# Other blocks for GpSimd's part of the softmax sums, and the steps that wait for GpSimd placed by an estimate of its queue

## The chip, the cores and the metric

The kernel runs on one core of a Trainium2 chip. The metric is the device time of one execution in microseconds, and the time of a version is the median of several runs. A core has engines that work side by side, each through its own queue of instructions in order: TensorE (matrix products; "PE" in the profile, with its weight loads as "PEld"), VectorE ("DVE"), ScalarE ("ACT"), GpSimd ("POOL") and SyncE ("SP", which here only starts transfers). TensorE writes to PSUM[...]. Transfers (DMA) started by SP and by GpSimd share 16 DMA engines.

## What is computed

`x` holds 8 frames of 2048 nodes with 256 channels. A transformer layer with 8 heads of 32 channels works within each frame, an adjacency matrix masks the scores, and the whole is wrapped in one more residual and norm:

```python
qkv = x @ w_qkv                                   # q, k, v of 8 heads, 32 channels each
scores = q k^T / sqrt(32), -1e9 where adj == 0
t = softmax(scores) @ v
y = layernorm(x + t) * g1 + be1                   # first norm
h = relu(y @ w1 + b1)
z = layernorm(y + h @ w2 + b2) * g2 + be2         # second norm
out = layernorm(x + z)                            # third norm, without gain
```

Per frame and head that is a matrix of 2048 x 2048 scores, so attention is nearly all of the work.

## The kernel before, in words

**Tiling.** For a frame `f`, a chunk `qc` of 512 query nodes and a half `g` of the heads (4 heads), the scores are made transposed, a block `mb` of 128 key nodes at a time. One such block is an *item*: 8 frames x 4 chunks x 2 halves x 16 blocks = 1024 items. 16 items of one `(f, qc, g)` are a *group*, 32 are a chunk, 128 are a frame. The main loop takes one item per step `t`. In a step it issues, in this order: fill work (`advance`), the exponential of item `t+1` on ScalarE (`exponentials`, L237), the score products of item `t+2` on TensorE and the mask's addition on VectorE (`scores`, L230 and L233), the products of item `t` with the values on TensorE (`values`, L249), and the summing of item `t` (`add_up`, L268 and L271).

**The tiles p.** VectorE writes an item's scores into a tile `p` of 1 MB (pool `pp`, 12 buffers), ScalarE turns them into exponentials in place, and TensorE multiplies them with the values. Each `p` is also a part of the softmax's denominator. A matrix product with ones (L315) sums over the key nodes of one `p` in 8 instructions, and to spare TensorE 12 of a group's 16 blocks, they are first added together elsewhere:
- GpSimd adds the blocks of `POOLED` into the first of them, by a tensor addition (L271), 6 per group;
- DMAs that add at their target fold the blocks of the two chains `MOVED` into the first block of each (L268), issued by GpSimd, 6 per group. One link of a chain waits until the link before it has landed, since both write the same tile, and that wait stands in GpSimd's queue;
- the block `ALONE` goes to TensorE as it is.

TensorE then takes four terms per group (`denominator`): `ALONE`, the heads of the two chains, and the head of `POOLED`. A tile `p` comes free when its last reader is done: GpSimd's addition, the DMA's landing, or TensorE's product.

**The chunk's rest.** When the denominators of both halves are there, `outcome` divides (L353), adds `x` by a DMA that GpSimd issues (L339), and `tail` follows: the first norm (statistics on VectorE L278, the power on GpSimd L283 to L287, the scaling on ScalarE L290), transposes and the two feed-forward products on TensorE, the gain and the bias rows on GpSimd (L459, L461), the residual's addition on VectorE (L483), the second norm, its gain and bias rows on GpSimd (L363, L365), the addition of `x` by a DMA from GpSimd (L367), the third norm, and the store from SP (L370). At most two tails are under way at once. The last chunk has a version of its own in halves (`finish`).

**What sets the order.** All of this is written as Python generators that a planner resumes when the program is built; nothing of it is decided on the chip. A generator yields a number of steps to stay away, or `BANK` when it wants TensorE and the one free PSUM bank for fill work. `advance` keeps a credit of TensorE time per step, so that about one piece of fill work (a term of a denominator, a projection, a transpose, a part of the feed-forward) goes into each step, and takes the piece that is due first. Where a generator stays away too short a time, its next instruction stands in its engine's queue before its operand is there, and that engine waits, with all that is behind it.

In the kernel before, these distances are fixed numbers: 2 steps from the power on GpSimd to the scaling on ScalarE, 7 steps from the DMA at L367 to the third norm, a start of the first norm 16 steps after the chunk's last item, and `SUM = 4` steps after a group's last item until the term of `POOLED`.

```python
    POOLED = (0, 3, 6, 8, 11, 13, 15)
    MOVED = ((1, 4, 7, 10), (2, 5, 9, 12))
    ALONE = 14
...
        late = {len(blocks) - 1: ready}
...
            start(t + 2, denominator(f, qc, g, t + SUM), t + SUM + 4)
```

Of the kernel before, what the change touches and what calls it, by code (L numbers as in the profile page):

```python
# [28 lines left out]
SUM_MAX = 1e19  # L29
BANK, MORE, WAIT, TURNED, ROOM, INPUTS = -1, -2, -3, -4, -5, -10  # L30
STEP, UNIT, TURN, KEPT = 2200, 1024, 1400, 2200

MASKED = -57344.0
CODE = -5.0
# [27 lines left out]
def fast_path(ctx, tc, cst, x, adj, out, RS):  # L62
    nc = tc.nc
    F, N, C = x.shape
# [18 lines left out]
    ctx.enter_context(tc.manual_schedule())  # L83

    ident, identb, wqkv, w1s, w2s = cst["ident"], cst["identb"], cst["wqkv"], cst["w1s"], cst["w2s"]
    state = {"pair": 0, "side": None, "turn": 0, "turned": False, "holder": None, "tails": 0, "credit": 0}

    def columns(out, lhsT, rhs, start, stop):
        state["credit"] -= 4 * out.shape[-1]
# [164 lines left out]

    POOLED = (0, 3, 6, 8, 11, 13, 15)
    MOVED = ((1, 4, 7, 10), (2, 5, 9, 12))
    ALONE = 14

    ENDED = MB - 5
    SUM = 4

    def add_up(item):
        f, qc, g, mb = item
        for chain in MOVED:
            if mb in chain[1:] and not ((f, qc, g) == items[-1][:3] and mb >= ENDED):
                nc.gpsimd.dma_start(PT[f, qc, g, chain[0]], PT.pop(item), accum_op=ALU.add)  # L268
        if mb in POOLED[1:] and not ((f, qc, g) == items[-1][:3] and mb >= ENDED):
            first = PT[f, qc, g, POOLED[0]]  # L270
            nc.gpsimd.tensor_tensor(first, first, PT.pop(item), ALU.add)  # L271


    def norm(t, per=1):
        mv = small.tile([P, TPC, nc.vector.BN_AGGR_DIM], F32, name="mv")
        for j in range(TPC):
            st = small.tile([P, nc.vector.BN_STATS_DIM], F32, name="st")
            nc.vector.bn_stats(st, t[:, j, :])  # L278
            nc.vector.bn_aggr(mv[:, j, :], st)
            if j % per == per - 1:  # L280
                yield 1
        rs = small.tile([P, TPC], F32, name="rs")
        nc.gpsimd.tensor_scalar(rs, mv[:, :, 1], EPS, 1.0, op0=ALU.add, op1=ALU.mult)  # L283
        nc.gpsimd.tensor_tensor(rs, rs, cst["mhalf"], ALU.pow)  # L284
        nb = small.tile([P, TPC], F32, name="nb")
        nc.gpsimd.tensor_tensor(nb, mv[:, :, 0], rs, ALU.mult)
        nc.gpsimd.tensor_scalar(nb, nb, -1.0, 1.0, op0=ALU.mult, op1=ALU.mult)  # L287
        yield 2
        for j in range(TPC):
            nc.scalar.activation(t[:, j, :], t[:, j, :], AF.Identity, bias=nb[:, j:j + 1], scale=rs[:, j:j + 1])  # L290
            if j % per == per - 1:
                yield 1
# [1 line left out]
    def rows(v):  # L294
        return v[:, None, :].to_broadcast([P, TPC, C])

    def denominator(f, qc, g, ready):
        grp = (f, qc, g)
        blocks = [ALONE] + [chain[0] for chain in MOVED + (POOLED,)]
        late = {len(blocks) - 1: ready}  # L300
        if (f, qc, g) == items[-1][:3]:
            blocks = [POOLED[0], 11, 12, MOVED[1][0], 13, 14, MOVED[0][0], 15]
            late = {n: len(items) - k for n, k in ((2, 2), (3, 1), (4, 1), (5, 0), (6, 0), (7, 0))}
        yield BANK
        ps = bank()
        for n, block in enumerate(blocks):
            if n:
                yield MORE
            while state["now"] < late.get(n, 0):
                yield WAIT  # L310
            term = PT.pop((f, qc, g, block))
            state["credit"] -= 4 * CH
            for h in range(4):
                r = D * h
                nc.tensor.matmul(ps[r:r + D, :], cst["ones"], term[:, h, :], start=(n == 0), stop=(n == len(blocks) - 1))  # L315
# [12 lines left out]
        nc.vector.tensor_tensor(RS[:, 1], RS[:, 1], den, ALU.min)  # L328
        if g == 1:
            begin = items.index((f, qc, g, LAST)) + SUM + 2  # L330
            start(begin, outcome(f, qc) if (f, qc) != (F - 1, NCK - 1) else finish(f, qc), begin)

    def outcome(f, qc):
        yield ROOM
        state["tails"] += 1
        xin = x[f, qc * CH:(qc + 1) * CH, :].rearrange("(p j) c -> p j c", p=P)
        y = yp.tile([P, TPC, C], F32, name="y")
        yield from divide(f, qc, y)
        nc.gpsimd.dma_start(y, xin, accum_op=ALU.add)  # L339
        begin = items.index((f, qc, 1, LAST)) + SUM + 2  # L340
        if (f, qc) == (F - 1, NCK - 2):
            start(begin + 5, tail(f, qc, y, xin, 2), begin + 8)
        else:
            start(begin + 10, tail(f, qc, y, xin), begin + 26)

    def divide(f, qc, y):
        rc = RC.pop((f, qc))
# [9 lines left out]
    def tail(f, qc, y, xin, per=1):  # L357
        yield from norm(y, per)
        yield from feed_forward(y)
        yield 1  # L360
        z = y
        yield from norm(z, per)
        nc.gpsimd.tensor_tensor(z, z, rows(cst["g2r"]), ALU.mult)  # L363
        yield 1
        nc.gpsimd.tensor_tensor(z, z, rows(cst["be2r"]), ALU.add)  # L365
        yield 1
        nc.gpsimd.dma_start(z, xin, accum_op=ALU.add)  # L367
        yield 7
# [68 lines left out]
    def finish(f, qc):  # L437
        y = yp.tile([P, TPC, C], F32, name="y")
        xr, xb = state["rows"]
        yield from divide(f, qc, y)  # L440
        yT, hT = (work.tile([P, 2, CH], F32, name=n) for n in ("turned", "hT"))
        dst = out[f, qc * CH:(qc + 1) * CH, :].rearrange("(p j) c -> p j c", p=P)
        both = [half_rows(h, y, xr, xb, yT, hT, dst) for h in range(2)]
        while both:
            for e in list(both):
                if next(e, both) is both:
                    both.remove(e)

    def feed_forward(y):
        yield TURNED  # L450
        state["turned"] = True
        yT = work.tile([P, 2, CH], F32, name="turned")
        for a in range(2):
            yield BANK
            ps = bank()
            transposes(ps, [y[:, j, a * P:(a + 1) * P] for j in range(TPC)])
            nc.scalar.activation(yT[:, a, :], ps, AF.Identity, bias=cst["be1c"][:, a:a + 1], scale=cst["g1c"][:, a:a + 1])
        yield 1
        nc.gpsimd.tensor_tensor(y, y, rows(cst["g1r"]), ALU.mult)  # L459
        yield 1  # L460
        nc.gpsimd.tensor_tensor(y, y, rows(cst["be1b2r"]), ALU.add)  # L461
        hT = work.tile([P, 2, CH], F32, name="hT")
        for d in range(2):
            yield BANK
            ps = bank()
            for a in range(2):
                if a:
                    yield MORE
                columns(ps, w1s[:, a, d * P:(d + 1) * P], yT[:, a, :], start=(a == 0), stop=(a == 1))
            nc.scalar.activation(hT[:, d, :], ps, AF.Relu, bias=cst["b1s"][:, d:d + 1], scale=1.0)  # L470
        state["turned"] = False
        yield 1
        z = y
        for jj in range(0, TPC, 2):
            yield BANK
            ps = bank()
            for j in range(jj, jj + 2):
                if j > jj:
                    yield MORE
                for d in range(2):  # L480
                    columns(ps[:, (j - jj) * C:(j - jj + 1) * C], hT[:, d, j * P:(j + 1) * P], w2s[:, d, :],
                            start=(d == 0), stop=(d == 1))
            nc.vector.tensor_tensor(z[:, jj:jj + 2, :], ps.rearrange("p (b c) -> p b c", c=C), z[:, jj:jj + 2, :], ALU.add)  # L483
# [115 lines left out]
    for t, (f, qc, g, mb) in enumerate(items):  # L599
# [9 lines left out]
            nc.sync.dma_start(xr, x[f, qc * CH:(qc + 1) * CH, :].rearrange("(p j) c -> p j c", p=P))  # L609
        if t == len(items) - 2:  # L610
            nc.gpsimd.tensor_tensor(xb, xr, rows(cst["be2r"]), ALU.add)
        if t:
            advance(t)

# [9 lines left out]
        values(items[t])  # L624
        add_up(items[t])
        if mb == LAST and t + 1 < len(items):
            start(t + 2, denominator(f, qc, g, t + SUM), t + SUM + 4)
        if t == len(items) - 3:
            start(t, denominator(f, qc, g, t), t)
    t = len(items)  # L630
    state["side"] = None
    while fill:
# [238 lines left out]
```

## Time and profile before

| what | value |
|---|---|
| time, median of 3 runs | 3244.03 us (3241.13 to 3246.06) |
| the profiled execution's own time | 3246.02 us |
| its span, first to last instruction | 3244.1 us |
| mean granted TensorE clock | 0.985 of full |
| VectorE busy | 2735.7 us (84%) |
| ScalarE busy | 2435.8 us (75%) |
| GpSimd busy | 2592.2 us (80%) |
| TensorE busy within 200 to 2940 us | 2702.77 of 2740 us |
| TensorE busy within 2940 to 3200 us | 234.23 of 260 us |

The span has three parts: up to about 97 us the masks, the first projections and transposes are prepared; then the 1024 steps; the last 45 us finish the last chunk. In the groups of instructions, a row gives the line, engine, operation and tiles, how many there were, their busy time and the mean of one; behind it stands how long the engine had been idle just before them, and who ended that idle time. In the view of waits, a row gives who waited for whom, the total in us, how often, and the longest. TensorE's matrix products overlap, so that eight of them, of 0.6 us each by the rows, pass in about 1 us.

### The profile page before, as it was taken

To read this page: it belongs to the slowest core of one execution; us is meant where nothing else is said; L and a number is where in the kernel's file an instruction comes from. 1 tells how busy PE (TensorE), PEld (TensorE's weight loads), DVE (VectorE), ACT (ScalarE), POOL (GpSimd) and SP (SyncE) were. 2 spreads that over 40 slices of the span, in tenths; PEclk is the share of its full clock that TensorE was granted. 3 is DMA by queue.
4 is the path that set the end of the run, shared out by engine and by line. 5 is a ranking of instruction groups with operands and counts; after the bars stand their busy time and mean duration, and the time that the engine had idled before them with its cause. 6 is when DMAs were issued, how large, how long until landed. Compare 5 with 4: busy or idle time off the path is not lost.

```text
span 3244.1 us, 68406 instructions
## 1 busy us (share of the span) xinstructions
PE 3109.4 (96%) x28996; PEld 979.0 (30%) x28996; DVE 2735.7 (84%) x3203; ACT 2435.8 (75%) x1941; POOL 2592.2 (80%) x1358
## 2 busy tenths in 40 slices
PE   7899999999999999999999999999999999998985
PEld 4222333223332233322233323323233323332222
DVE  4888888888888888888988888888888888888975
ACT  3667778777777777778777778777778777777774
POOL 0568888888878888788887888888888788878884
PEclk8899999999999999999999999999999999999998
DMA  9688779778879788788787879878788878877763
GB/s 320 145 181 185 183 176 199 178 177 196 181 176 207 171 188 193 159 195 200 178 181 174 185 174 221 177 167 198 173 192 197 177 168 198 181 171 161 166 145 86
DMA packets 153240, 590.52 MB, mean 182 GB/s; under 512 B 15040, under 2 KB 67776, under 8 KB 103904
## 3 DMA queue, kind: packets, MB, share of 16 engines
q0 software_dynamic: 64416, 434.80, 66.9%
q1 hardware_dynamic: 87696, 149.98, 13.1%
q8 instruction: 229, 3.75, 0.4%
q10 hardware_dynamic: 816, 1.31, 0.1%
q14 instruction: 83, 0.68, 0.1%
HBM read 146.67 MB, written 37.75 MB: 57 GB/s over the span
## 4 chain that ended last, share of the span: by engine, by line
PE 75%; DVE 7%; POOL 5%; issue 4%; DMA 4%; ACT 2%; DVEq 0%; POOLq 0%; ACTq 0%
PE s L230 27%; PE x L249 24%; PE x L54 14%; PE x L315 6%; DVE p L233 6%; PE x L95 4%; DMA p<-p 3%; POOL p L271 2%; ACT p L237 1%; DMA mask<-md 1%; POOL y L365 1%; DVE st L278 1%; POOL y L363 0%; POOL y L461 0%; POOL y L459 0%
## 5 line engine op out<-in xcount | busy, mean ns | idle before, releaser
L233 DVE TENSOR_TENSOR p<-s,mask 128x1024 f32<-128x1024 f32 x2048 | 2409.3, 1218 | 372.7 <-PE s L230 209.9
L237 ACT ACTIVATE p<-p 128x2048 f32<-128x2048 f32 x1024 | 1956.1, 1910 | 521.4 <-DVE p L233 465.6
L271 POOL TENSOR_TENSOR p<-p 128x2048 f32<-128x2048 f32 x381 | 1825.5, 4793 | 223.7 <-ACT p L237 221.3
L230 PE MATMUL s<-qT,kT 32*128 32x512 f32 x8192 | 1173.8, 643 | 40.8 <-DVE p L233 35.9
L249 PE MATMUL x<-p,v 128*32 128x512 f32 x8192 | 1096.0, 607 | 16.7 <-ACT p L237 16.4
L268 POOL DMA_DIRECT2D p<-p x383 | 359.3, 956 | 306.9 <-ACT p L237 88.3
L230 PEld LDWEIGHTS s<-qT,kT 32*128 32x128 f32 x8192 | 321.1, 183 | 644.7 <-DVE p L233 587.2
L249 PEld LDWEIGHTS x<-p,v 128*32 128x32 f32 x8192 | 161.6, 108 | 797.8 <-issue 310.6
L315 PE MATMUL x<-p,ones 128*32 128x512 f32 x2080 | 268.2, 594 | 17.9 <-POOL p L271 11.1
L290 ACT ACTIVATE y<-y,nb,rs 128x256 f32<-128x256 f32 x372 | 218.7, 590 | 40.4 <-POOL nb L287 40.4
L54 PE MATMUL x<-in,wqkv 128*32 128x512 f32 x1888 | 243.5, 592 | 0.0
L278 DVE BATCH_NORM_STATS2 st<-y 128x6 f32<-128x256 f32 x372 | 154.9, 416 | 5.1 <-DMA y<-in_x_dram 5.1
L54 PE MATMUL x<-turned,w1s 128*32 128x512 f32 x992 | 123.5, 596 | 0.4 <-ACT in L166 0.4
L54 PE MATMUL x<-w2s,hT 128*32 128x256 f32 x2016 | 121.8, 382 | 2.1 <-DVE y L483 2.1
L54 PEld LDWEIGHTS x<-wqkv,in 128*32 128x32 f32 x3584 | 102.2, 110 | 63.4 <-issue 58.9
L315 PEld LDWEIGHTS x<-p,ones 128*32 128x32 f32 x2080 | 66.3, 110 | 178.2 <-issue 140.4
L54 PE MATMUL x<-wqkv,in 128*32 128x128 f32 x3584 | 117.3, 273 | 0.0
L54 PEld LDWEIGHTS x<-in,wqkv 128*32 128x32 f32 x1888 | 61.7, 110 | 140.9 <-issue 113.7
L284 POOL TENSOR_TENSOR rs<-rs,mhalf 128x4 f32<-128x4 f32 x93 | 96.3, 1036 | 7.8
L54 PEld LDWEIGHTS x<-w2s,hT 128*32 128x32 f32 x2016 | 65.4, 111 | 75.0 <-issue 33.0
L363 POOL TENSOR_TENSOR y<-y,g2r 128x1024 f32<-128x1024 f32 x31 | 82.5, 2663 | 5.3 <-ACT y L290 5.3
L461 POOL TENSOR_TENSOR y<-y,be1b2r 128x1024 f32<-128x1024 f32 x31 | 83.0, 2679 | 0.6
(116 smaller groups left out, 1335.7 us busy)
## 6 DMA issues: line engine op xcount, KB each, us to landing
p<-p POOLq DMA_DIRECT2D x383, 1024.0 KB, 10.4
in<-xd SPq DMA_DIRECT2D x87, 512.0 KB, 10.6
mask<-md SPq DMA_DIRECT2D x248, 128.0 KB, 7.9
y<-in_x_dram POOLq DMA_DIRECT2D x62, 512.0 KB, 8.1
p<-in_adj_dram SPq DMA_DIRECT2D x16, 1024.0 KB, 10.7
out_dram<-y SPq DMA_DIRECT2D x31, 512.0 KB, 6.2
in<-in_x_dram SPq DMA_DIRECT2D x29, 512.0 KB, 15.5
xd<-in SPq DMA_DIRECT2D x28, 512.0 KB, 11.2
```

The costliest lines, as they stand in the source:

```text
L54: nc.tensor.matmul(out[r:r + D], lhsT[:, r:r + D], rhs, start=start, stop=stop)
L95: nc.tensor.transpose(ps[:, j * P:(j + 1) * P], s, ident)
L230: nc.tensor.matmul(ps2[half][:, j, :], KT[f, mb // TPC, g][r:r + D, (mb % TPC) * P:(mb % TPC + 1) * P], QT[f, qc, g][r:r + D, :], start=Tr ...
L233: nc.vector.tensor_tensor(pt[:, 2 * half:2 * half + 2, :], ps, MK[f, qc, mb // 2][:, mb % 2, None, :].to_broadcast([P, 2, CH]), ALU.add)
L237: nc.scalar.activation(PT[item], PT[item], AF.Exp, scale=1.0 / math.sqrt(D))
L249: nc.tensor.matmul(O[grp][r:r + D, :], V[f, mb // TPC, g][:, mb % TPC, r:r + D], PT[item][:, h, :], start=(mb == 0), stop=(mb == LAST))
L268: nc.gpsimd.dma_start(PT[f, qc, g, chain[0]], PT.pop(item), accum_op=ALU.add)
L271: nc.gpsimd.tensor_tensor(first, first, PT.pop(item), ALU.add)
L278: nc.vector.bn_stats(st, t[:, j, :])
L284: nc.gpsimd.tensor_tensor(rs, rs, cst["mhalf"], ALU.pow)
L290: nc.scalar.activation(t[:, j, :], t[:, j, :], AF.Identity, bias=nb[:, j:j + 1], scale=rs[:, j:j + 1])
L315: nc.tensor.matmul(ps[r:r + D, :], cst["ones"], term[:, h, :], start=(n == 0), stop=(n == len(blocks) - 1))
```

## The change

GpSimd now sums blocks 0, 1, 3, 5, 8, 10 and 12; the DMA chains are 2, 6, 9, 13 and 4, 7, 11, 14; block 15 goes to TensorE as it is. The planner keeps an estimate, in steps, of when GpSimd's queue will have worked off what was given to it (`state["pool"]`, advanced by `queue`), and of when each of the three sums of a group will be ready (`ends`). Norms, the tail's start, the residual's addition and the terms of the denominators are placed no earlier than this estimate with a reserve of 0.6 steps (`SPARE`). The terms of a denominator are taken in the order of their estimated times, and each waits for its own. In the last group some blocks and their order change accordingly. In `finish`, each round over the last chunk's two halves is followed by a yield of one step, so that other generators are resumed between the rounds.

```diff
+ADD, ISSUE, ROWS, POWER, LINK, LAND = 1.65, 0.32, 0.92, 0.56, 2.8, 2.5
+SPARE = 0.6
...
+    ends = {}
+
+    def queue(length, ready=0.0):
+        state["pool"] = max(state["pool"], state["now"], ready) + length
+        return state["pool"]
+
+    def until(ready, least=1):
+        return max(least, math.ceil(ready + SPARE - state["now"]))
...
-    POOLED = (0, 3, 6, 8, 11, 13, 15)
-    MOVED = ((1, 4, 7, 10), (2, 5, 9, 12))
-    ALONE = 14
+    POOLED = (0, 1, 3, 5, 8, 10, 12)
+    MOVED = ((2, 6, 9, 13), (4, 7, 11, 14))
+    ALONE = 15
...
                 nc.gpsimd.dma_start(PT[f, qc, g, chain[0]], PT.pop(item), accum_op=ALU.add)
+                first = f, qc, g, chain[0]
+                ends[first] = queue(ISSUE, ends.get(first, 0.0)) + LINK
         if mb in POOLED[1:] and not ((f, qc, g) == items[-1][:3] and mb >= ENDED):
             first = PT[f, qc, g, POOLED[0]]
             nc.gpsimd.tensor_tensor(first, first, PT.pop(item), ALU.add)
+            ends[f, qc, g, POOLED[0]] = queue(ADD)
...
         nc.gpsimd.tensor_scalar(nb, nb, -1.0, 1.0, op0=ALU.mult, op1=ALU.mult)
-        yield 2
+        yield until(queue(POWER), 2)
...
-    def denominator(f, qc, g, ready):
-        grp = (f, qc, g)
-        blocks = [ALONE] + [chain[0] for chain in MOVED + (POOLED,)]
-        late = {len(blocks) - 1: ready}
+    def sums(grp):
+        blocks = sorted([ALONE] + [chain[0] for chain in MOVED + (POOLED,)], key=lambda b: ends.get(grp + (b,), 0.0))
+        return blocks, [ends.get(grp + (b,), 0.0) + SPARE for b in blocks]
+
+    def denominator(f, qc, g):
+        blocks, late = sums((f, qc, g))
+        late = dict(enumerate(late))
         if (f, qc, g) == items[-1][:3]:
-            blocks = [POOLED[0], 11, 12, MOVED[1][0], 13, 14, MOVED[0][0], 15]
+            blocks = [POOLED[0], MOVED[0][0], 11, 12, 13, MOVED[1][0], 14, 15]
...
         nc.gpsimd.dma_start(y, xin, accum_op=ALU.add)
+        landed = state["now"] + until(queue(ISSUE) + LAND)
         begin = items.index((f, qc, 1, LAST)) + SUM + 2
         if (f, qc) == (F - 1, NCK - 2):
-            start(begin + 5, tail(f, qc, y, xin, 2), begin + 8)
+            start(landed, tail(f, qc, y, xin, 2), begin + 12)
         else:
-            start(begin + 10, tail(f, qc, y, xin), begin + 26)
+            start(landed, tail(f, qc, y, xin), begin + 26)
...
         nc.gpsimd.tensor_tensor(z, z, rows(cst["g2r"]), ALU.mult)
+        queue(ROWS)
         yield 1
         nc.gpsimd.tensor_tensor(z, z, rows(cst["be2r"]), ALU.add)
+        queue(ROWS)
         yield 1
         nc.gpsimd.dma_start(z, xin, accum_op=ALU.add)
-        yield 7
+        yield until(queue(ISSUE) + LAND)
...
         nc.gpsimd.tensor_tensor(y, y, rows(cst["g1r"]), ALU.mult)
+        queue(ROWS)
         yield 1
         nc.gpsimd.tensor_tensor(y, y, rows(cst["be1b2r"]), ALU.add)
+        ready = queue(ROWS)
...
         state["turned"] = False
-        yield 1
+        yield until(ready - 1)
...
         if mb == LAST and t + 1 < len(items):
-            start(t + 2, denominator(f, qc, g, t + SUM), t + SUM + 4)
+            begin = max(t + 2, math.ceil(max(e - n for n, e in enumerate(sums((f, qc, g))[1]))))
+            start(begin, denominator(f, qc, g), begin + 6)
...
                 if next(e, both) is both:
                     both.remove(e)
+            yield 1
```

More of the change, by code (lines that the diff above doesn't have):

```diff
@@ L85, in fast_path @@
     ident, identb, wqkv, w1s, w2s = cst["ident"], cst["identb"], cst["wqkv"], cst["w1s"], cst["w2s"]
-    state = {"pair": 0, "side": None, "turn": 0, "turned": False, "holder": None, "tails": 0, "credit": 0}
+    state = {"pair": 0, "side": None, "turn": 0, "turned": False, "holder": None, "tails": 0, "credit": 0,
+             "now": 0, "pool": 0.0}
+    ends = {}
[4 more added lines that the diff above has]
+        return max(least, math.ceil(ready + SPARE - state["now"]))
     def columns(out, lhsT, rhs, start, stop):
@@ L330, in denominator @@
             begin = items.index((f, qc, g, LAST)) + SUM + 2
-            start(begin, outcome(f, qc) if (f, qc) != (F - 1, NCK - 1) else finish(f, qc), begin)
+            start(state["now"] + 1, outcome(f, qc) if (f, qc) != (F - 1, NCK - 1) else finish(f, qc), begin)
     def outcome(f, qc):
@@ L611, in fast_path @@
             nc.gpsimd.tensor_tensor(xb, xr, rows(cst["be2r"]), ALU.add)
+        state["now"] = t
         if t:
@@ L626, in fast_path @@
         if mb == LAST and t + 1 < len(items):
-            start(t + 2, denominator(f, qc, g, t + SUM), t + SUM + 4)
+            begin = max(t + 2, math.ceil(max(e - n for n, e in enumerate(sums((f, qc, g))[1]))))
+            start(begin, denominator(f, qc, g), begin + 6)
         if t == len(items) - 3:
-            start(t, denominator(f, qc, g, t), t)
+            start(t, denominator(f, qc, g), t)
     t = len(items)
```

## The prediction

> **What bounds the kernel now.** I read the page first (busy times, groups), then the waits of TensorE, of ScalarE and of the whole core, then the timeline around single waits. The page:
>
> ```profile
> PE 3109.4 (96%) x28996; PEld 979.0 (30%) x28996; DVE 2735.7 (84%) x3203; ACT 2435.8 (75%) x1941; POOL 2592.2 (80%) x1358
> ...
> L271 POOL TENSOR_TENSOR p<-p 128x2048 f32<-128x2048 f32 x381 | 1825.5, 4793 | 223.7 <-ACT p L237 221.3
> L268 POOL DMA_DIRECT2D p<-p x383 | 359.3, 956 | 306.9 <-ACT p L237 88.3 <-issue 80.9 <-DMA p<-p 75.5
> ...
> p<-p POOLq DMA_DIRECT2D x383, 1024.0 KB, 10.4
> ```
>
> TensorE is the bound; GpSimd is next to it in need of exact timing, since its work comes in pieces of 4.8 us. What a change of order can win is TensorE's waits, between 200 and 2940 us:
>
> ```profile
> PE x L249 <- ACT p L237: 11.1, 8, 2.2
> PE x L315 <- POOL p L271: 11.1, 6, 2.1
> PE s L230 <- DVE p L233: 7.5, 20, 0.4
> PE x L315 <- DMA p<-p: 2.9, 4, 1.3
> PE x L54 <- DVE y L483: 2.1, 4, 0.9
> ```
>
> Row 2 and 4 are terms of denominators that come before GpSimd's or a DMA's sum is there. Row 5 is the residual's addition behind GpSimd's bias row. Row 3 are 20 steps without fill work, where VectorE sets the pace. Row 1 looks like ScalarE, but the timeline shows what it is (GpSimd, then ScalarE, then TensorE):
>
> ```profile
> 1427.29 0.86 POOL L268 DMA_DIRECT2D p<-p  x1 [7.21 <-issue]
> 1427.85 4.88 POOL L271 TENSOR_TENSOR p<-p 128x2048 f32<-128x2048 f32 x1
> 1434.73 0.60 ACT L290 ACTIVATE y<-y,nb,rs 128x256 f32<-128x256 f32 x1 [4.05 <-POOL nb L287]
> 1437.18 1.07 PE L249 MATMUL x<-p,v 128*32 128x512 f32 x8 [2.19 <-ACT p L237]
> ```
>
> GpSimd stood 7.2 us on a chain's link (the link before it had not landed), then did an addition, then the norm's power; ScalarE stood 4.05 us on that norm with the next exponential behind it; TensorE lost 2.19 of these, so about 1.9 us of such a stall are absorbed. Towards the end the same happens larger: 5.06 us at 2996.89, and here, where VectorE stands on the landing of y:
>
> ```profile
> 3128.36 0.43 DVE L278 BATCH_NORM_STATS2 st<-y 128x6 f32<-128x256 f32 x1 [5.13 <-DMA y<-in_x_dram]
> 3130.80 2.09 PE L230 MATMUL s<-qT,kT 32*128 32x512 f32 x8 [6.52 <-DVE p L233]
> 3132.82 1.94 PE L249 MATMUL x<-p,v 128*32 128x512 f32 x8
> ```
>
> After that wait TensorE runs at half pace for three groups (2.09, 1.94 and 1.92 us, where the same groups take 1.14 and 1.07): (2.09 - 1.14) + (1.94 - 1.07) + (1.92 - 1.14) = 2.6 us more.
>
> [...] the norm at 1434.73 holds up the exponential behind it. [...] The trace shows 10.4 us to landing; I use that.
>
> **The change, part by part.**
>
> *Work.* The instructions as built have the same products on TensorE (8 x 1024 for scores and for values, 2080 for denominators). GpSimd does 383 additions for 381 and issues 381 links for 383: +2 x 4.79 - 2 x 0.96 = +7.7 us, both in the last group, beside the scores of that group. Additions of blocks 8 to 10 and the rows between them (2 x 4.79 + 2 x 2.65 + 0.96 = 15.8 us, norm included about 17.7) have from step 1016 to step 1022, in which the order as built puts steps of 2 x 2.65 and 4 x 3.8 = 20.5 us: hidden by 2.8 us, and a wait for the rest if it is late. Zero taken.
>
> *Waits in the middle.* Rows 1, 2, 4 and 5: 11.1 + 11.1 + 2.9 + 2.1 = 27.2 us. All four come from distances that ignore GpSimd's queue, and these become estimates. How good are they? A step is 2740 us by 906 items (7248 products of values by 8) = 3.02 us. ADD 1.65 is then 4.98 us (row: 4.79), ROWS 0.92 is 2.78 (rows: 2.55 to 2.69), POWER 0.56 is 1.69 (0.19 + 1.04 + 0.20 + 0.20 = 1.63, with gaps 1.9 in the timeline), LINK 2.8 is 8.5 (10.4 - 0.96 = 9.4: short by 1.0). SPARE adds 1.8 us and covers that. It does not cover a landing far above the median (the longest is 17.5 us), nor several steps in a row with a transpose (2.65 us each, where ADD is worth 4.4). I take 80% as won: -21.8; bounds 40% and 100%, -10.9 and -27.2.
>
> *Blocks.* In the old queue a link three blocks after its forerunner comes three times per group (4-7, 7-10, 9-12), in the new one twice (6-9, 11-14), the second with nothing behind it until block 1 of the next group. The last addition moves from block 15 to 12, so the last sum is now a chain: link 14 at step 14, ready 14 + 0.32 + 2.8 + 0.6 = 17.7; its term stands at the fourth place, step 20 at the earliest. When GpSimd is on time that leaves 2.3 steps, 6.9 us.
>
> *Waits at the end.* The norm at 2996 (5.1) and the landing at 3130 (6.5 + 2.6): 14.2 us. The norm that stood on y at 2 steps' distance from the division now has 4; 4 x 2.65 = 10.6 us stand against a landing of 9.5 there plus about 2.5 us until the issue. Some of it may stay: -12, bounds -5 and -14.
>
> *Wait at the start.* 3.9 us at 195 us, behind a link that took 15 us to land. The estimate does not know of it: 0 taken.
>
> *Fill.* In the order as built, steps without fill work go from 62 to 66. Such a step costs 2.49 us (start to start, at 103.77 and 106.26), its work 2/3 of a full step of 2.93, 1.95: 4 x 0.54 = +2.2.
>
> *Tiles p.* A tile's buffer is taken again some steps after its reader was issued. By the addresses as built, additions with 4 steps between go from 7 to 34, those with 3 from 13 to 9; links with 3 or 4 from 26 to 12. An addition takes 1.65 steps and VectorE writes 0.7 into the step (2.2 us in the timeline), so 4 steps bear a lag of 3.05 steps = 9.2 us, 3 bear 6.2. The first addition of a group now lags its exponential by 0.5 us in the median, 7.6 at most, above 6.2 in 3 of 63 groups. Behind VectorE stand all masks, then exponentials, then TensorE. I take +3; bounds 0 and the second rival.
>
> *Finish.* GpSimd's row L363 (2.4 us) now stands between the two halves of the last chunk and pushes the second half's statistics by about 1 us, in a chain with no cover: +1. Longer tails (4 to 6 steps instead of 3 from statistics to scaling) cost nothing: other fill work stands in these steps, and the store waits alone.
>
> **Sum:** -21.8 - 12 + 2.2 + 3 + 1 = -27.6 us. The profiled execution took 3246.0 us for a span of 3244.1, and the median is 3244.0, so the saving is taken off the median: 3216 us.
>
> **Rivals.**
> 1. *The estimate is a step short.* Denominators and norms wait as before, in other places; only the end is won: -12 + 2.2 + 3 + 1 + about 2 = -4, 3240 us. For it: LINK is short of the measured landing, and short steps make every figure short. Against: SPARE is larger than the miss.
> 2. *GpSimd becomes the bound* (slower). Its additions, issues and the norms fill 2288 of 2740 us, and 14 - 11 = 3 blocks of distance (9.1 us) are less than a link's 10.4 us, so a late queue stands on links at 9 and 14 and grows later. If an early addition in a group lags by 11 us, its buffer with 4 steps is 1.8 us late, VectorE waits, and TensorE after it. In the 32 groups of frames 2 to 5, where the planner itself spreads the norms most: 32 x 1.8 = 58 us, 3216 + 58 = 3274. It decides from 28/32 = 0.9 us per group on, that is a lag of 10.1 us. Against: the lag at a group's last addition is 7.7 us in the median and 12.5 at most now, and it is gone by the next group's first.
> 3. *All waits go*, the one at the start too: -27.2 - 14.2 - 3.9 - 2.5 (its slow pace after) + 2.2 = -45.6, 3198 us.
>
> **How the numbers follow.** Likeliest 0.60, alone 3199 to 3235; rival 1 0.14; rival 2 0.14; rival 3 0.12. A change of 0.2% (6.5 us) is about what a measurement here tells from none. Faster: the likeliest but for 0.02, rival 3, and 0.03 of rival 1, 0.73; same: 0.11 of rival 1 and 0.01 of the rest, 0.12; slower: rival 2 and 0.01, 0.15. Range: 3196, just under rival 3, to 3258, which takes in rival 1 and the lower half of rival 2.
>
> **What would show it.** In the profile after, in the waits of TensorE: products of denominators on GpSimd's additions and on DMAs under 5 us together, products of values on ScalarE under 5, no wait above 4 us between 2900 and 3195; ScalarE's wait for the norms' scalars (now 30.5 us in the middle) under 10; busy times of all engines unchanged within 1%. Wrong if VectorE is seen to wait for GpSimd or for chain landings before it writes p (now 2.0 and 1.7 us), or if GpSimd's idle time before its additions falls towards nothing.

## The result, and the profile after

The changed kernel takes 3292.31 us (median of 6 runs, 3289.12 to 3298.56), the kernel before beside it 3243.5 us (6 runs, 3238.87 to 3246.06). The ratio is 1.0156, 95% interval 1.0145 to 1.0167: about 49 us slower, where 3216 us was forecast.

The profiled execution has a span of 3287.7 us for 3244.1. These 43.6 us divide in two: TensorE is busy 12.7 us longer (3122.1 for 3109.4, with the same 28996 products) and idle 30.9 us longer (span less busy: 165.6 for 134.7). The page of the changed kernel (engine totals; the additions of GpSimd; the issues of links and of the loads into y with KB and the median time to landing):

```profile
PE 3122.1 (95%) x28996; PEld 979.9 (30%) x28996; DVE 2740.8 (83%) x3203; ACT 2439.5 (74%) x1941; POOL 2599.3 (79%) x1358
...
L286 POOL TENSOR_TENSOR p<-p 128x2048 f32<-128x2048 f32 x383 | 1830.0, 4778 | 242.8 <-ACT p L250 159.6
...
p<-p POOLq DMA_DIRECT2D x381, 1024.0 KB, 10.7
...
y<-in_x_dram POOLq DMA_DIRECT2D x62, 512.0 KB, 8.7
```

The work is what it was: VectorE, ScalarE and GpSimd are busy within 7.1 us of before, an addition takes 4.78 us for 4.79. What changed is who waits. TensorE's waits from 200 to 2940 us of the changed kernel (total us, number, longest):

```profile
PE s L243 <- DVE p L246: 46.9, 51, 4.5
PE x L334 <- DMA p<-p: 19.4, 13, 3.2
PE x L108 <- DVE y L373: 3.4, 4, 2.9
PE x L57 <- ACT kT L202: 1.4, 2, 0.7
PE x L57 <- DVE y L508: 0.3, 1, 0.3
```

The five rows of before add up to 34.7 us, these to 71.4. The two rows of 11.1 us (values behind ScalarE's norm, denominators behind GpSimd's additions) are gone, as the change says. In their place stand scores behind VectorE's masks (46.9 for 7.5) and denominators behind a link (19.4 for 2.9). The waits of VectorE over the whole span say what its masks stood behind:

```profile
DVE st L294 <- DMA y<-in_x_dram: 29.0, 10, 5.1
DVE p L246 <- DMA p<-p: 23.2, 16, 3.0
...
DVE y L373 <- DMA out_dram<-y: 3.4, 1, 3.4
DVE p L246 <- POOL p L286: 3.0, 4, 1.4
```

The first two of these in the kernel before (the one wait for y lies at its end):

```profile
DVE st L278 <- DMA y<-in_x_dram: 5.1, 1, 5.1
...
DVE p L233 <- DMA p<-p: 1.7, 1, 1.7
```

If each of TensorE's waits for the masks in the changed kernel (69.9 us over the whole span) is paired with the longest wait of VectorE in the 3.5 us before it, 23.2 us of them stand behind a load into y and 10.6 us behind a link at a tile p. So three things are late in the changed kernel: a load into y at its norm, a link at the tile p that it frees, and a link at the term that it sums. Here is one of each. First y, in the timeline (start, us, engine, line, idle before and what ended it):

```profile
813.37 0.43 DVE L294 BATCH_NORM_STATS2 st<-y 128x6 f32<-128x256 f32 x1 [4.86 <-DMA y<-in_x_dram]
...
815.22 2.09 PE L243 MATMUL s<-qT,kT 32*128 32x512 f32 x8 [4.32 <-DVE p L246]
...
817.24 1.94 PE L262 MATMUL x<-p,v 128*32 128x512 f32 x8
```

The statistics stand 4.86 us for the landing, the mask addition behind them in VectorE's queue comes late, TensorE loses 4.32 us and then runs these two groups at half pace, and most of the next (1.65 us for 1.04): (2.09 - 1.14) + (1.94 - 1.06) + (1.65 - 1.04) = 2.4 us more. Of the 29.0 us, 21.1 are first loads (L358, 7 waits) and 7.9 second ones (L389, 3 waits). Then the links of one chain's end:

```profile
2592.09 1.89 POOL L281 DMA_DIRECT2D p<-p  x1
...
2602.59 0.86 POOL L281 DMA_DIRECT2D p<-p  x1 [8.61 <-DMA p<-p]
...
2607.97 1.20 PE L334 MATMUL x<-p,ones 128*32 128x512 f32 x8 [2.71 <-DMA p<-p]
...
2613.31 1.06 PE L334 MATMUL x<-p,ones 128*32 128x512 f32 x8 [0.62 <-DMA p<-p]
```

The last link stands in GpSimd's queue until the link before it on the same tile has landed, 10.5 us after that one's issue (2602.59 - 2592.09); its own landing then releases the term at 2613.31, 10.7 us on. Two landings in series, 21 us. And a tile p, which VectorE may write only when the link that reads it has landed:

```profile
1177.38 2.35 DVE L246 TENSOR_TENSOR p<-s,mask 128x1024 f32<-128x1024 f32 x2 [2.58 <-DMA p<-p]
...
1178.66 1.14 PE L243 MATMUL s<-qT,kT 32*128 32x512 f32 x8 [0.65 <-DVE p L246]
```

### The profile page after: what moved, and what is told of

Same layout as the page of the kernel before. It is cut to its first block, busy times and chain, and to the rows that moved or that the text cites. A ratio compares the mean times of both kernels' runs of the same rounds, so it can differ in the third digit from the quotient of the medians.

```text
span 3287.7 us, 68434 instructions
## 1 busy us (share of the span) xinstructions
PE 3122.1 (95%) x28996; PEld 979.9 (30%) x28996; DVE 2740.8 (83%) x3203; ACT 2439.5 (74%) x1941; POOL 2599.3 (79%) x1358
## 4 chain that ended last, share of the span: by engine, by line
PE 47%; DMA 12%; DVE 7%; POOL 4%; issue 3%; ACT 2%; DVEq 0%; POOLq 0%; ACTq 0%
PE s L243 17%; PE x L262 15%; DMA p<-p 10%; PE x L57 10%; DVE p L246 6%; PE x L334 4%; POOL p L286 2%; DMA y<-in_x_dram 2%; PE x L108 2%; ACT p L250 1%; DVE st L294 1%; POOL y L386 0%; POOL p L281 0%; POOL y L383 0%; DMA out_dram<-y 0%
## 5 line engine op out<-in xcount | busy, mean ns | idle before, releaser
L243 PE MATMUL s<-qT,kT 32*128 32x512 f32 x8192 | 1180.5, 646 | 74.4 <-DVE p L246 69.9
L281 POOL DMA_DIRECT2D p<-p x381 | 382.9, 1038 | 324.8 <-DMA p<-p 92.0
L334 PE MATMUL x<-p,ones 128*32 128x512 f32 x2080 | 270.2, 597 | 26.8 <-DMA p<-p 26.6
L336 ACT COPY dT<-x 128x512 f32<-128x512 f32 x64 | 37.5, 586 | 66.7 <-PE x L334 66.6
L57 PEld LDWEIGHTS x<-w2s,hT 128*32 128x32 f32 x2016 | 65.5, 111 | 71.4 <-issue 36.0
## 6 DMA issues: line engine op xcount, KB each, us to landing
p<-p POOLq DMA_DIRECT2D x381, 1024.0 KB, 10.7
in<-xd SPq DMA_DIRECT2D x87, 512.0 KB, 10.5
```

The source lines that it names most:

```text
L57: nc.tensor.matmul(out[r:r + D], lhsT[:, r:r + D], rhs, start=start, stop=stop)
L243: nc.tensor.matmul(ps2[half][:, j, :], KT[f, mb // TPC, g][r:r + D, (mb % TPC) * P:(mb % TPC + 1) * P], QT[f, qc, g][r:r + D, :], start=Tr ...
```

## The experiments

Four theories were tried. A: tails start too early for y's landing. B: a chain's last link lands after the step that the estimate gives its term. C: tiles p are held too long, by late links and late terms. D (formed after the second group of runs): a norm put off by the estimate puts off the store of y, and with two tiles y the division of the chunk after next stands on that store. All medians stand beside 3240 to 3242 us of the kernel before, timed on the same chip with each group. Runs built on the kernel before keep the changed kernel's yield of one step in `finish`.

| run | edit | us | ratio, 95% |
|---|---|---|---|
| e1_land | changed kernel, landing 4.5 steps | 3293.4 | 1.0170, 1.0153 to 1.0187 |
| e2_late | changed, chain's terms one step later | 3272.8 | 1.0097, 1.0079 to 1.0116 |
| e6_tails | changed, starts of tails and 7 steps before the last norm as before | 3333.8 | 1.0285, 1.0266 to 1.0304 |
| e4_blocks | before, with the new blocks | 3369.7 | 1.0394, 1.0377 to 1.0412 |
| e7_norms | before, with norms and residual by estimate | 3272.7 | 1.0095, 1.0073 to 1.0116 |
| e8_late_land | e1 and e2 together | 3270.3 | 1.0087, 1.0068 to 1.0106 |
| e8_late2_land | the same, terms two steps later | 3291.3 | 1.0150, 1.0131 to 1.0168 |
| e10_norms_tails | e7 with tails by estimate | 3342.0 | 1.0312, 1.0288 to 1.0335 |
| e11_z5 | e7, 5 steps for the second load | 3257.4 | 1.0052, 1.0034 to 1.0071 |
| e12_z5_den | e11, additions' term by estimate | 3260.5 | 1.0059, 1.0041 to 1.0077 |
| e14_blocks_z5 | e6 and e2, 5 steps for the second load | 3323.3 | 1.0266, 1.0241 to 1.0291 |
| e16_cap3 | e7, a norm waits 3 steps at most | 3246.7 | 1.0018, 1.0011 to 1.0026 |
| e16_cap3z6 | the same, 6 steps for the second load | 3245.4 | 1.0014, 1.0008 to 1.0021 |
| e17_blocks_room | e6 and e2, two steps after the store | 3276.1 | 1.0104, 1.0089 to 1.0118 |

### What the changed kernel's own estimates cost

**Landing at 4.5 steps.**

```diff
-ADD, ISSUE, ROWS, POWER, LINK, LAND = 1.65, 0.32, 0.92, 0.56, 2.8, 2.5
+ADD, ISSUE, ROWS, POWER, LINK, LAND = 1.65, 0.32, 0.92, 0.56, 2.8, 4.5
```

> The changed kernel with the landing of y or z priced at 4.5 steps (13.6 us) for 2.5 (7.6 us). Theory A (the tail now starts a landing's estimate after the issue, the estimate is short of the 9.7 us that the load takes in the median plus its 2 to 3 us until issue, and VectorE stands on y with the mask additions behind it): VectorE's wait for y's landing falls from 29.0 us to under 6, TensorE's wait on VectorE's masks from 69.9 to under 50, and the time from 3292 to 3250 to 3262. Theory B (denominators' terms come before a chain's sum has landed) and theory C (tiles p come free late, because links land late): the wait for y goes all the same, but the time stays within 8 us of 3292.

Measured 3293.4 us, no gain. VectorE's wait for y is gone, its wait on tiles p fell from 23.2 to 6.5 us, and scores behind the masks fell by 34.5 us, as theory A says. But the denominators' wait on links doubled. TensorE's waits of this run, whole span:

```profile
PE x L334 <- DMA p<-p: 56.2, 23, 4.9
PE s L243 <- DVE p L246: 35.4, 74, 1.4
...
PE x L108 <- DMA in<-in_x_dram: 8.0, 3, 2.8
```

In the changed kernel the same rows read 26.6 and 69.9, and the third is absent. -34.5 + 29.6 + 8.0 is 3 us: the wait moved to another place. So y's early norm was real, but not what the 49 us come down to: with it gone, the terms come before their links more often. Perhaps a stall of VectorE had been giving the links time; that is argued, and shown is only that the one wait replaced the other. Theory A falls as an account of the whole.

**A chain's term one step later.**

```diff
-        return blocks, [ends.get(grp + (b,), 0.0) + SPARE for b in blocks]
+        return blocks, [ends.get(grp + (b,), 0.0) + SPARE + (b in (2, 4)) for b in blocks]
```

> The changed kernel with one step (3.0 us) more before the denominator's term of a chain, nothing else changed in the estimates. Theory B: TensorE's wait of denominators on links falls from 26.6 us to under 10, and the time to 3270 to 3280. Theory A: that wait may fall, the time stays above 3282, since the landing of y costs the most. Theory C: a tile p that waits for its term is held a step longer, VectorE's wait on tiles p rises above its 23.2 us and the time is 3290 or more.

Measured 3272.8 us, 20 us less than the changed kernel. TensorE's waits, whole span:

```profile
PE s L243 <- DVE p L246: 64.1, 84, 3.6
PE x L334 <- DMA p<-p: 15.7, 10, 2.5
```

The time is what theory B gave, though the wait fell to 15.7 us and not under 10. The estimate of the links was too short, and one step more for their terms alone gives back 20 of the 49 us. Of the 18.2 us by which the span is shorter, TensorE waits 10.9 less and is busy 7.3 less (3114.8 us for 3122.1). The wait on links fell by 10.9, but other rows moved too: VectorE's wait for y went from 29.0 to 17.9 us, and TensorE's for the masks from 69.9 to 64.1. VectorE's wait on tiles p stayed (25.1 us for 23.2), so one step more held them hardly longer.

**Both, and two steps.** The edits of the two runs above together; then `2 * (b in (2, 4))`.

> The changed kernel with both corrections: 4.5 steps for a landing and one step more before a chain's term. Alone the first took away VectorE's wait and moved it to the chains' terms (26.6 to 56.2 us), the second gave 20 us. Theory B with A: the terms' waits are 23 of 2.4 us in the mean and 4.9 at most, one step takes most of them: under 15 us, time 3235 to 3250. Theory C: tiles p are then held too long, VectorE's wait on them rises above 20 us, time 3265 or more.

> The same with two steps more before a chain's term. Theory B: the terms' waits under 5 us, 3230 to 3245. Theory C: each step more holds two tiles p longer; VectorE's waits on tiles p rise over those with one step, and the time is 10 us or more above it.

Measured 3270.3 and 3291.3 us. With one step, y's wait is gone again and brings 2.5 us at most (the two intervals overlap), and the time misses what B with A gave by 20 us: the terms' wait is 17.8 us, the residual now stands for GpSimd's bias row (36.7 us of VectorE) and the tiles p are as late as ever. With two steps, the links are practically always there (5.0 us of TensorE's wait), and the tiles are not. VectorE's waits in the run with one step, then with two:

```profile
DVE y L508 <- POOL y L485: 36.7, 13, 3.4
DVE p L246 <- DMA p<-p: 26.5, 16, 4.0
```

```profile
DVE p L246 <- DMA p<-p: 65.9, 32, 5.9
```

Theories B and C are both right, and they bound each other: a term too early waits for its link, a term one step too late holds its tiles and more than doubles VectorE's wait on them (39 us more wait, 21 us more time). With 12 tiles p, none of the three settings tried (no step more, one, two) makes both small.

**The starts of tails.** In the changed kernel, as the kernel before has them (the last chunk but one likewise, not shown):

```diff
-            start(landed, tail(f, qc, y, xin), begin + 26)
+            start(begin + 10, tail(f, qc, y, xin), begin + 26)
 ...
-        yield until(queue(ISSUE) + LAND)
+        queue(ISSUE)
+        yield 7
```

> The changed kernel with the starts of tails as in the kernel before (16 steps after the chunk's last block, 11 in the last chunk but one, and 7 steps from the last load to its norm); blocks, norms and denominators as changed. Theory A: as with the longer landing, 3252 to 3265, VectorE's wait for y under 8 us for 29.0. B and C: 3284 to 3300.

Measured 3333.8 us, 41 us slower than the changed kernel, which no theory expected: the wait for y falls to 8.1 us, and the denominators' wait on links rises from 26.6 to 75.1 us. It is an exchange like that with the longer landing, and a larger one.

### The blocks alone, and the estimates alone

**New blocks in the kernel before**, with the additions' sum second and the chains after it, the last term still 4 steps late (the list of the last group, not shown, is the changed kernel's):

```diff
-    POOLED = (0, 3, 6, 8, 11, 13, 15)
-    MOVED = ((1, 4, 7, 10), (2, 5, 9, 12))
-    ALONE = 14
+    POOLED = (0, 1, 3, 5, 8, 10, 12)
+    MOVED = ((2, 6, 9, 13), (4, 7, 11, 14))
+    ALONE = 15
 ...
-        blocks = [ALONE] + [chain[0] for chain in MOVED + (POOLED,)]
+        blocks = [ALONE] + [chain[0] for chain in (POOLED,) + MOVED]
```

> The kernel before with the new blocks alone (in the denominator the additions' sum second and the two chains after it, the wait of 4 steps before the last term kept), none of the estimates. Theory A: the blocks are worth little, 3243 within 8 us. Theory B: the later chain is not there at its term, TensorE's wait of denominators on links rises from 6.9 to some 20 us, 3255 to 3265. Theory C: VectorE's wait on tiles p for a link rises from 1.7 us to some 20, and the time to 3258 to 3275.

Measured 3369.7 us: 128 us slower. TensorE's waits, whole span:

```profile
PE x L315 <- DMA p<-p: 105.6, 39, 5.9
PE s L230 <- DVE p L233: 50.7, 68, 9.4
```

Before, the first was 6.9 us. The direction is B's, the wait five times the 20 us that it gave; VectorE's waits on tiles p (15.7 us for links, 16.0 for additions) are there too, as C says. The traces give the times of the links, here for the 62 groups between the first and the last. Block 14's link of the changed kernel is issued 7.4 us after its exponential's end and lands 19.8 us after it (medians; longest 29.1). In the kernel before, the last link is block 12's and lands 19.1 us after its exponential; the last sum is the addition of block 15, which starts 7.7 us after its exponential and takes 4.8, so it is there at 12.5 us. Counted from block 14's exponential with a step of 3.0 us, the additions' sum was there after 15.5 us and block 12's link after 13.1; now the last sum is there after 19.8.

**Norms and residual by estimate, in the kernel before.** The two lines that make the wait (the queue's bookkeeping and the yield in `finish` come with them; blocks, denominators and starts of tails are those of before):

```diff
-        yield 2
+        yield until(queue(POWER), 2)
 ...
-        yield 1
+        yield until(ready - 1)
```

> The kernel before (its blocks, its denominators, its starts of tails) with the estimates for the norms' power and for the bias row before the residual alone. If the 80% of the prediction hold for this part (values on ScalarE 11.1, the residual's 2.1, the norm of 5.1 at the end): 3220 to 3230 for 3241, ScalarE's wait on the norms 40.4 to under 5, denominators' waits on additions and links as before (11.1 and 6.9). The rival, that a norm put off keeps y and the tail's later work waiting: 3241 or more.

Measured 3272.7 us, 32 us slower, where 11 to 21 us of gain were expected from the very part of the change whose effect is plainest. ScalarE's wait on the norms is gone, and so are TensorE's waits behind it and those on additions. A wait of 9.5 us of TensorE on the load of the next inputs is new. Above all, VectorE's divisions now stand on the store of y, and TensorE on these. TensorE's row and VectorE's row of this run:

```profile
PE x L108 <- DVE y L373: 38.3, 7, 5.8
```

```profile
DVE y L373 <- DMA out_dram<-y: 43.9, 8, 6.4
```

One of the seven in the timeline (store, division, next division's transposes, next scores):

```profile
684.70 0.34 SPq L393 DMA_DIRECT2D out_dram<-y  x1
...
693.26 0.69 DVE L373 TENSOR_TENSOR y<-x,rc 128x512 f32<-128x512 f32 x1 [5.76 <-DMA out_dram<-y]
...
694.01 1.13 PE L108 MATMUL x<-ident,oT 128*128 128x128 f32 x4 [5.18 <-DVE y L373]
...
695.14 2.09 PE L243 MATMUL s<-qT,kT 32*128 32x512 f32 x8
```

In the order as built, the third norm of one chunk in four waits 6 steps for 2, so its store is issued in the very step in which the chunk after next divides. Both use one of the two tiles y. That is theory D.

**Tails by estimate on top of it**, that is, the kernel before with everything but the blocks and the denominators:

> The kernel before (blocks and denominators) with the estimates for norms, the residual and the tails' starts, the landing at 2.5 steps. Theory A in the narrow form (the early tail costs by itself): VectorE's wait for y 20 to 30 us and 15 to 35 us above the run with the norms alone. If the early tail costs only together with the late chains: within 8 us of the run with the norms alone.

Measured 3342.0 us, 69 us above e7. Not as expected: VectorE's wait for y is 6.9 us only, and the cost is elsewhere: 31.1 us of TensorE's wait on additions and 19.6 on links in denominators whose fixed step no longer suits, 23.0 us of VectorE's wait on tiles p, 20.9 on the store. With the old blocks and terms at a fixed step the early tails cost 69 us, with the new blocks and terms by estimate they save 41 (e6): the price of this part depends on the others.

### Whether the store of y is the cause of the 32 us

**Second load at 5 steps for 7** (the store comes two steps earlier), then **the additions' term by estimate** as well:

```diff
-        yield 7
+        yield 5
```

```diff
-        late = {len(blocks) - 1: ready}
+        late = {len(blocks) - 1: max(ready, ends.get((f, qc, g, POOLED[0]), 0.0) + SPARE)}
```

> The kernel before with the estimates for norms and residual, as in the run of them alone, and 5 steps for 7 between the last load and its norm. Theory D (a norm put off puts off the store of y, and with two tiles y the division of the chunk after next stands on VectorE until that store has landed: 43.9 us there, 38.3 us of TensorE's divisions behind it): two steps earlier that wait is under 8 us and the time 3220 to 3236. If the 32 us were due to something else that the estimates move: 3260 or more.

> The same, and the last term of a denominator (the additions' sum, block 15's the last) put off to the estimate of GpSimd's queue where that is later than 4 steps. If the estimate is good: denominators' wait on additions from 11.1 to under 4 us, 6 to 12 us faster than the run without it. Theory C: a later term holds four tiles p longer, VectorE's wait on tiles p rises above 10 us, and the time is equal or longer.

Measured 3257.4 and 3260.5 us. The wait on the store is gone and 15 us with it, less than expected, for the second load now lands after its norm's statistics are due (VectorE, first run):

```profile
DVE st L294 <- DMA y<-in_x_dram: 37.8, 13, 5.3
```

The seventh and sixth step were in use: in the kernel before, the seven shortest distances from that landing to its statistics are 1.0 to 2.0 us. In the second run the denominators' wait on additions stays at 11.1 us for 10.5. Its edit did almost nothing: TensorE's products stand in the same order in both traces but for one term, at 3169 us, that comes two steps later. So the estimate of the queue is almost never later than the 4 steps that stood there and cannot take these waits away, and the 3 us between the two runs are hardly its effect.

**A norm's wait limited to 3 steps**, with 7 and with 6 steps for the second load:

```diff
-        yield until(queue(POWER), 2)
+        yield min(until(queue(POWER), 2), 3)
```

> The kernel before with the estimates for norms and residual, a norm's wait at most 3 steps (without the limit it is 6 in one chunk of four, and that chunk's store is issued in the very step in which the chunk after next divides). Theory D: VectorE's wait for the store falls from 43.9 us to under 5, the landings before the last norm keep their 7 steps (5.2 us of wait, as in the run without the limit), TensorE's waits on ScalarE stay under 5 us: 3222 to 3236. If the store is not the cause: 3260 or more.

> The same with 6 steps for 7 from the last load to its norm. The six shortest distances from landing to norm were 0.8 to 2.2 us at 7 steps, a step is 3.0 us: some six waits of 1 to 2 us for VectorE, 0 to 8 us slower than with 7 steps if theory D's mechanism holds for loads too; 20 us or more slower if a landing is as costly as with 5 steps (37.8 us of wait there).

Measured 3246.7 and 3245.4 us: of the 32 us, 26 and 27 are gone with the wait on the store. Two different edits, an earlier load and a shorter norm, take that wait away and bring time with it, so theory D is shown. The forecast gain (3222 to 3236) did not come. TensorE's waits on additions (11.1 us) went, but the norms that needed more steps stand on ScalarE again (20.6 us of TensorE's wait behind them, where under 5 was expected), and 9.1 us of TensorE's wait on the load of the next inputs is new. ScalarE's row, 40.4 us in the kernel before, in the first run:

```profile
ACT y L306 <- POOL nb L303: 47.4, 7, 7.9
```

For these seven norms no place that was tried is good: at 2 or 3 steps ScalarE waits, at 6 the store does (4 and 5 were not tried). With 6 steps for the second load the time is 1.3 us lower, within the two intervals. VectorE's wait for y is then 20.6 us, with twelve waits of 0.6 to 1.8 us where six were expected, and it reached TensorE: its wait for the masks rose from 40.7 to 55.2 us, while that behind ScalarE fell from 20.6 to 8.7.

### What the new blocks cost when the rest is put right

Both runs take the changed kernel's blocks, norms and denominators, one step more before a chain's term, and the starts of tails as before. The first has 5 steps for the second load; the second has 7, and this:

```diff
+        yield 2
         state["tails"] -= 1
```

> The changed kernel with its blocks and denominators, one step more before a chain's term, the starts of tails as before and 5 steps for 7 before the last norm: against the run before it, the new blocks and their denominators are the difference. Theory B: the new blocks' last link is issued at block 14 and lands 19.8 us after its exponential in the median, where the old blocks' last sum is done 12.5 us after block 15's, so the new blocks cost by themselves, 20 us or more over that run. Theory A (the loss is in the starts of tails): within 8 us of that run.

> The changed kernel with one step more before a chain's term, the starts of tails as before (7 steps before the last norm), and two steps between the store of y and the release of its place. If the changed kernel's loss over the terms' 20 us lay in the starts of tails and y's store: 3240 to 3255. If the new blocks hold tiles p too long by themselves (theory C): VectorE's wait on tiles p stays above 20 us and the time is 3265 or more.

Measured 3323.3 and 3276.1 us. The first is 63 us above the run with the old blocks (e12), but 58.0 us of wait for y in it, for 36.3 there, mix into that, so it settles nothing alone. The second has 3.1 us of wait on the store left, and 24.1 us on y, all of it on first loads. VectorE's waits in it:

```profile
DVE p L246 <- DMA p<-p: 48.1, 26, 3.8
...
DVE st L294 <- DMA y<-in_x_dram: 24.1, 13, 7.7
```

The nearest run with the old blocks is e16_cap3 (VectorE's wait on tiles p for links 1.8 us, on y 5.3). Against it the new blocks cost 3276.1 - 3246.7 = 29 us, though the treatment is not the same: there a norm's wait is limited, here the store has two steps of room. The lowest two times with the new blocks, 3270.3 and 3272.8, are 24 and 26 us above that run. So some 25 to 30 us go with the blocks and their denominators in the versions tried. Paired as above, 26.7 us of TensorE's waits for the masks in e17 stand behind a link at a tile p, for 0.3 in e16_cap3, and 19.7 behind a load into y, for 6.7. That the tiles p are the larger part of the cost rests on these waits; a kernel with a thirteenth tile p was not tried. No version ran faster than the kernel before.

## Why the prediction was wrong

**The step that failed first: "link 14 at step 14, ready 14 + 0.32 + 2.8 + 0.6 = 17.7".** The sum lets the last link start in its own step, prices one landing at 8.5 us, and says of the shortfall: "SPARE adds 1.8 us and covers that." The trace of the changed kernel (medians of the same 62 groups) has link 14 start 7.4 us after its block's exponential. It stands in GpSimd's queue for the link before it: in 57 groups it starts within 0.7 us of link 11's landing. Link 11 is itself issued 4.4 us after its exponential and takes 10.7 us; link 14 then takes 11.6, where issue and LINK give 0.32 + 2.8 steps, 9.4 us. So the last sum is there 19.8 us after the exponential, where the prediction had 3.7 steps, 11.2 us, with the reserve in it. Of "2.3 steps, 6.9 us" of slack the median group has 2.5 us left, in 10 groups the last term stands and waits (18.0 us), and in 5 the term before it (8.6 us). Rival 2 had the fact, three blocks of distance are less than one link's landing, but charged it to the additions only. One step more for these terms is 20 us less.

**Waits in the middle, -21.8.** The named rows did what was said: 11.1 + 11.1 + 2.1 became 0.3. Row 4, counted as a gain of up to 2.9, became a loss of 16.5 for the reason above. What was omitted is that VectorE's own waits, for y and for tiles p, reach TensorE through row 3: "20 steps without fill work" grew from 7.5 to 46.9.

**y's landing.** The prediction reckoned 4 steps against a landing and the time to issue for the end only ("Some of it may stay"), and not for the other 30 chunks, although the change gives all of them the same estimate: 7.6 us for a load that takes 9.3 us in the median there and up to 15.7. That is 29.0 us of VectorE's time, and 23.2 of TensorE's (6.5 in the kernel before). Yet the longer landing alone gained nothing, so even a right entry there would not have given the sum: the waits exchange with those for links.

**Tiles p, +3.** It was argued from the additions, and for these it holds (3.0 us of wait for 2.0). The links were counted by distance ("from 26 to 12", a relief) without their later issue and landing. They cost VectorE 23.2 us for 1.7. TensorE's waits behind them come to 10.6 us. The rival that ended slower, 3274, had this mechanism with the wrong releaser.

**"Longer tails (4 to 6 steps instead of 3 from statistics to scaling) cost nothing: other fill work stands in these steps, and the store waits alone."** Behind the store waits the next user of its tile (VectorE's divisions for 43.9 us in e7_norms). In the kernel before, these longer norms alone cost 32 us, of which 26 went when their wait was limited and the store came in time. In the changed kernel the wait on the store is 3.4 us, so this did not make the 49 (that the early tails hide it is argued); it shows that taking away that row, -11.1 in the forecast, brought no time by itself in any run.

**End, -12, and finish, +1.** TensorE's waits in the last 304 us go from 34.9 to 31.3, 3.6 less where 12 were forecast. The norm's 5.1 is gone, the masks' wait is 14.0 for 20.0, a term's wait of 3.7 is new, and the finish is 4.2 us longer for 1 (7.3 and 4.8 for 5.2 and 2.7).

**Pace.** The sum has no entry for it in the middle, though it came there too after short waits, in the kernel before as well: there TensorE ran at about half pace after waits of 1.90 us (eight products in 1.91 us for 1.07) and 2.00 us (1.97 for 1.14). From 200 to 3200 us the traces record the granted clock at half in 11 stretches, 44.4 us together, for 4 and 17.1 before. By an estimate from these and from the doubled times, the 27.3 us more would cost 13.7 if TensorE were busy all through them; it was busy 12.7 us longer.

**What holds.** GpSimd's additions and rows, the order of the blocks at the end and the cost of the extra work were sized right, and GpSimd's busy time is as summed. What was listed as making it wrong (VectorE waiting for GpSimd or a landing before it writes p) is what the profile shows.

## What to carry to other kernels

Taking a wait away by putting an instruction off is not free (the norms put off in e7_norms cost 32 us): before pricing it, list what the later instruction holds (a tile, a buffer, a store's source) and who takes that next, and count the gain only where that next user has slack in the trace. An estimate of a queue has to be taken at the trace's landing time, with the spread and with links in series counted one after another, since the margin that covered one link here (1.8 us of reserve) was used up by the second, which started 7.4 us after its exponential. Where tiles are few, "too early" and "too late" may leave no good step at all, which a run with one step more and one with two more shows quickly.

## What the runs showed of the hardware

Whether TensorE runs at half pace after a wait does not go by the length of the wait alone. In the changed kernel eight score products took 2.09 us after a wait of 2.44 us and 1.14 us, the usual time, after one of 2.68 us; in the kernel before they took 1.97 us soon after a wait of 2.00 us (start, us, idle before; the first fence is of the changed kernel):

```profile
1070.41 1.14 PE L243 MATMUL s<-qT,kT 32*128 32x512 f32 x8 [2.68 <-DVE p L246]
...
1469.08 2.09 PE L243 MATMUL s<-qT,kT 32*128 32x512 f32 x8 [2.44 <-DVE p L246]
1471.10 1.55 PE L262 MATMUL x<-p,v 128*32 128x512 f32 x8
```

```profile
1111.04 1.07 PE L315 MATMUL x<-p,ones 128*32 128x512 f32 x8 [2.00 <-POOL p L271]
1112.03 1.97 PE L230 MATMUL s<-qT,kT 32*128 32x512 f32 x8
```

What else it depends on is left open. In the changed kernel each of the 11 stretches at half clock between 200 and 3200 us cost 1.4 to 2.7 us on top of the wait (the products' time beyond their usual one, as in the sums above).

A 1 MB link from SBUF to SBUF took 6.8, 10.7 and 19.5 us to landing (shortest, median, longest) in the changed kernel, and a 512 KB load into y at L358 5.7, 9.3 and 15.7: the longest is nearly three times the shortest, so a fixed step before either was wrong for some of them.
